# A graph-attention kernel that loads edge features and receivers for two groups of quads at once

## The chip, the cores and the metric

The kernel runs on one core of a Trainium2 chip. The core has a matrix engine (TensorE, called PE in the profile), a vector engine (VectorE, DVE), an activation engine (ScalarE, ACT), a general engine (GpSimd, POOL) and SyncE (SP), which here only issues transfers. Each engine works through its own instructions in order. Transfers run on sixteen DMA engines that all queues share. The metric is the time of one execution on the device, in microseconds (us), lower is better.

## The reference

`x` holds 6250 nodes with 128 features in 8 heads of 16. There are 206250 edges; `src` names the sender and `dst` the receiver, and the edges come sorted by `dst`. The reference is one message-passing layer with a residual and a layer norm:

```
w   = silu(edge_attr_32    @ rad_W1 + rad_b1) @ rad_W2 + rad_b2      # per edge, 128 wide
    + silu(edge_attr_32_n2 @ sph_W1 + sph_b1) @ sph_W2 + sph_b2
q   = (x @ Wq)[dst]         k = (x @ Wk)[src]         v = (x @ Wv)[src]
alpha = sum over a head of (q * w * k) / sqrt(16) * edge_weight      # one per edge and head
out = segment_sum(alpha * v, dst) / 16
result = layernorm(x + out)
```

## The kernel before, in words

**Tiles.** 128 edges are a tile, four tiles a quad (512 edges), four quads a group (2048 edges). There are 101 groups (`NG`) and 403 quads. Because the edges are sorted by receiver, the receivers of one quad lie in a window of 32 nodes, and those of a group in a window of 128. A receiver is kept as its place in the quad's window (`rel`).

**Start.** The kernel computes K and V of every node and stores them as one table in HBM, `kv_tab`, with rows of 1 KB. Beside this it turns `rel` around with TensorE (`relT`), so that the edges of a tile lie along a row, and stores it to HBM: first as `rel_lin`, then, read back with every row repeated four times, as `rel_four` (`store_rel`, lines 477 to 486). `store_rel` is called twice: once for the first 128 tiles (8 groups), early, and once for the rest, at the end of the start. The start also issues the loads for the first groups (lines 541 to 545) and the first gathers.

**The loop** (lines 808 to 881) runs over groups and in each over four slots, one quad a slot, in the order 0, 2, 1, 3. At slot i TensorE computes the first layers of quad i+2 (`first_layers`, line 560, which reads `feats`), the queries at the edges of quad i+1 (line 579, a matmul with the one-hot `hotT`, which DVE makes from `relb`, line 292) and the second layers of quad i+1 (line 612). ACT applies silu (line 597). DVE multiplies q, k and w (lines 628 to 641), and weighs v (line 653). TensorE then sums messages by receiver (line 664).

**K and V rows.** They come by sender from `kv_tab`. Four gathers of 128 rows each on POOL (line 141) bring a quad's rows, issued 14 quads ahead. In 60 of the quads ("row quads", about every 6.55 quads: slots `8 + (n + 1) * 393 // 60`) the fourth tile does not come by a gather: its 128 rows are 128 single transfers of 1 KB into the tile `wide`, 60 issued by SP and 68 by ACT (line 214), after the row addresses have been read into registers (line 208). `load_rows` spreads each row quad's transfers over the slots ahead of it; the last ones stand five slots ahead of the quad in program order. DVE waits for all 128 at line 625 before it starts on the quad at line 628.

**SP's program.** Besides the rows, SP issues for each group: the features `feats` (line 252, 512 KB, in slot 3), the receivers `relb` (line 263, 128 KB, in slot 2), the window of nodes `x` (line 315, 64 KB, in slot 0, behind an address load at line 310 every four groups), and the output `y` (line 773, 64 KB). `feats` has three buffers and `relb` four, and both are loaded three groups ahead. A load of `feats` waits for a signal of TensorE from two slots earlier (`mark`), so that its buffer is free. All of SP's instructions run one after another, so each stands in line with the rows.

Of the kernel before, what the change touches and what calls it, by code (L numbers as in the profile page):

```python
# [12 lines left out]
F32 = mybir.dt.float32  # L13
BF16 = mybir.dt.bfloat16
# [11 lines left out]
P = 128  # L26
# [6 lines left out]
GT = 16  # L33
QT = 4
NQ = GT // QT
NG = math.ceil(E / (P * GT))
NT = NG * GT
EG = P * GT
EQ = P * QT
QUADS = math.ceil(E / EQ)  # L40
NB = math.ceil(N / P)
NBC = 7
ROWS = (NB + 1) * P
W = 32
# [28 lines left out]
def gnn_kernel(ctx, tc, x, src, dst, weight, edges, rad_W1, rad_b1, rad_W2, rad_b2,  # L73
# [14 lines left out]
    nc = tc.nc  # L88
    const = ctx.enter_context(tc.tile_pool(name="const", bufs=1))
    dram = ctx.enter_context(tc.tile_pool(name="dram", bufs=1, space=DRAM))  # L90

    kv_tab = dram.tile([NB * P, 2 * D], F32, name="kv_tab")
    rel_lin = dram.tile([NT, P], BF16, name="rel_lin")
    rel_four = dram.tile([NT // QT, NQ, EQ], BF16, name="rel_four")
    acc = dram.tile([ROWS, D], F32, name="acc")
# [31 lines left out]
    gp = ctx.enter_context(tc.tile_pool(name="group", bufs=2))  # L127
# [45 lines left out]
    feats_of, relb_of, act_of, kv_of, hot_of, hotT_of, x_of, q_of, msg_of = ({} for _ in range(9))  # L173
# [75 lines left out]

    def load_feats(g, mark=None):  # L250
        feats_of[g] = gp.tile([P, EG // 2], F32, name="feats", bufs=3)
        o = nc.sync.dma_start(feats_of[g], edges[g])
        if mark is not None:
            tc.add_manual_dep(o.ins, mark.ins.name, WAIT, reason="one signal of TensorE a quad")
# [3 lines left out]

    def load_rel(g, pool, bufs):

        relb_of[g] = pool.tile([P, EQ], BF16, name="relb", bufs=bufs)
        r = rel_four[g * NQ:(g + 1) * NQ].rearrange("j n e -> (j n) e")
        nc.sync.dma_start(relb_of[g], r[:, None, :].to_broadcast([NQ * NQ, W // NQ, EQ]))

# [74 lines left out]
    with tc.tile_pool(name="nodes", bufs=1) as nodes, \  # L339
# [136 lines left out]

        def store_rel(a, b):
            for i, n in ((slice(a, min(b, NT // P)), P), (slice(NT // P, b), NT % P)):
                if i.start < i.stop:
                    t = slice(i.start * P, i.start * P + (i.stop - i.start) * n)  # L480
                    nc.sync.dma_start(rel_lin[t, :].rearrange("(n p) e -> p n e", p=n), relT[:n, i, :])
            a, b = a * P // QT, min(b * P, NT) // QT
            r = rel_lin.rearrange("(q t) e -> q (t e)", t=QT)
            for a, b in ((a, b - b % (P // 8)), (b - b % (P // 8), b)):
                if a < b:
                    nc.sync.dma_start(rel_four[a:b], r[a:b, None, :].to_broadcast([b - a, NQ, EQ]))

# [13 lines left out]
        n = len(chunks)  # L501
# [17 lines left out]
        for i, (k, n) in enumerate(work):  # L519
# [20 lines left out]
            if i == len(chunks) - 1:  # L540
                load_rel(0, gp, 1)
                load_feats(0)
                for g in range(1, XL):
                    load_x(g)
                    load_feats(g)
                nc.sync.dma_start(scale, weight)
        for q in order[XQ:AHEAD]:
            gathers(q)
        nc.vector.tensor_tensor(bsum, b2[:, 0:1], b2[:, 1:2], op=OP.add)
        store_rel(1, math.ceil(NT / P))  # L550
        nc.vector.tensor_scalar(scale, scale, SCALE, None, op0=OP.mult)


    with tc.tile_pool(name="ps", bufs=1, space=PSUM) as pp, tc.tile_pool(name="loop", bufs=1) as lp:
# [242 lines left out]

        written, ready, ready_at = [], [], []
        load_rel(1, lp, 4)
        load_rel(2, lp, 4)  # L800
        silus(order[0], first_layers(order[0]))
# [6 lines left out]
        for g in range(NG - 1):  # L808
            for slot, j in enumerate((0, 2, 1, 3)):
# [34 lines left out]
                if slot == 0:  # L844
                    if g + XL < NG:
                        load_x(g + XL, past)
                if slot == 3 and g + 3 < NG:
                    load_feats(g + 3, past)
                if slot == 2 and g + 3 < NG:
                    load_rel(g + 3, lp, 4)  # L850
                if slot == 0 and 1 <= g:
# [256 lines left out]
```

## Time and profile before

| | us |
|---|---|
| three runs | 2588.82, 2596.52, 2597.5 (median 2596.52) |
| the profiled execution | 2599.59 |
| its span, first to last instruction | 2597.7 |
| PE busy | 2090.8 |
| DVE busy | 1525.9 |
| POOL busy | 1470.8 |
| ACT busy | 645.0 |

The span is the time from the first to the last instruction of the profiled execution. SP has no busy time in this table, because instructions that issue transfers are not counted as busy; what SP does has to be read from the order of its instructions in time and from what waits for it. The clock that TensorE was granted was 0.837 of full speed on average.

### The profile page before, as it was taken

To read this page: it belongs to the slowest core of one execution; us is meant where nothing else is said; L and a number is where in the kernel's file an instruction comes from. 1 tells how busy PE (TensorE), PEld (TensorE's weight loads), DVE (VectorE), ACT (ScalarE), POOL (GpSimd) and SP (SyncE) were. 2 spreads that over 40 slices of the span, in tenths; PEclk is the share of its full clock that TensorE was granted. 3 is DMA by queue.
4 is the path that set the end of the run, shared out by engine and by line. 5 is a ranking of instruction groups with operands and counts; after the bars stand their busy time and mean duration, and the time that the engine had idled before them with its cause. 6 is when DMAs were issued, how large, how long until landed. Compare 5 with 4: busy or idle time off the path is not lost.

```text
span 2597.7 us, 56700 instructions
## 1 busy us (share of the span) xinstructions
PE 2090.8 (80%) x15990; PEld 1744.9 (67%) x15990; DVE 1525.9 (59%) x3427; ACT 645.0 (25%) x1359; POOL 1470.8 (57%) x1564
## 2 busy tenths in 40 slices
PE   5678888888888788878888878888887888888787
PEld 4567677666767666666667667666766767676666
DVE  3456556656656555656656556555656556565567
ACT  1122222222222222222222222222222222222223
POOL 4456565655565565555556555555555555565540
PEclk7788888888888888888888797888788787887888
DMA  5543444434343343434434434444343343443331
GB/s 180 173 118 112 120 124 116 121 112 122 113 123 116 116 124 114 120 112 122 121 111 123 119 114 121 115 120 121 114 120 118 111 122 115 119 124 108 118 103 35
DMA packets 157219, 307.18 MB, mean 118 GB/s; under 512 B 42022, under 2 KB 91360, under 8 KB 156896
## 3 DMA queue, kind: packets, MB, share of 16 engines
q0 software_dynamic: 73984, 201.43, 27.2%
q1 hardware_dynamic: 72976, 97.35, 11.4%
q10 hardware_dynamic: 9936, 4.72, 0.8%
q8 instruction: 127, 2.08, 0.3%
q14 instruction: 196, 1.61, 0.2%
HBM read 289.88 MB, written 15.11 MB: 117 GB/s over the span
## 4 chain that ended last, share of the span: by engine, by line
PE 38%; issue 20%; SPq 13%; DVE 13%; another core or an unknown queue 10%; ACTq 5%; ACT 1%; DMA 0%; DVEq 0%
PE pw L612 17%; SPq L214 10%; PE pq L579 7%; PE ph L560 6%; ACTq L214 4%; PE po L664 3%; DVE kq L628 3%; DVE side L638 2%; DVE kq L636 2%; SPq L208 2%; PE pq L705 1%; ACT act L597 1%; PE pk L381 1%; PE pq L286 1%
## 5 line engine op out<-in xcount | busy, mean ns | idle before, releaser
L141 POOL DMA_INDIRECT kv<-kv_tab,src_i x1520 | 1436.9, 945 | 1042.9 <-remote 447.9
L612 PE MATMUL pw<-w,act 128*128 128x128 f32 x6448 | 1060.4, 324 | 109.1 <-issue 107.6
L612 PEld LDWEIGHTS pw<-w,act 128*128 128x128 f32 x6448 | 951.7, 231 | 187.0 <-issue 149.7
L597 ACT ACTIVATE act<-ph,b 128x512 f32<-128x512 f32 x806 | 554.7, 689 | 1843.5 <-remote 1374.7
L628 DVE TENSOR_TENSOR kq<-pq,kv 128x512 f32<-128x512 f32 (+1 forms) x404 | 270.6, 670 | 931.3 <-remote 680.0
L560 PE MATMUL ph<-feats,w 32*128 32x512 f32 x1612 | 665.7, 740 | 138.5 <-issue 128.8
L579 PE MATMUL pq<-q,hotT 32*128 32x128 f32 x3224 | 557.5, 321 | 20.9 <-issue 17.8
L579 PEld LDWEIGHTS pq<-q,hotT 32*128 32x128 f32 x3224 | 470.7, 220 | 33.0 <-issue 32.7
L560 PEld LDWEIGHTS ph<-feats,w 32*128 32x128 f32 x1612 | 190.7, 207 | 303.6 <-issue 272.0
L638 DVE TENSOR_REDUCE side<-kq 128x32 f32<-128x512 f32 x404 | 280.2, 694 | 14.0
L653 DVE TENSOR_TENSOR msg<-kv,side 128x512 f32<-128x512 f32 (+1 forms) x404 | 268.7, 665 | 13.9
L636 DVE TENSOR_TENSOR kq<-pw,kq 128x512 f32<-128x512 f32 x404 | 274.1, 679 | 0.0
L664 PE MATMUL po<-msg,hot 128*32 128x128 f32 x3200 | 183.2, 309 | 34.2 <-issue 34.1
L567 PE MATMUL pw<-brow,onesb 3*128 3x512 bf16 x403 | 176.5, 438 | 0.0
L664 PEld LDWEIGHTS po<-msg,hot 128*32 128x32 f32 x3200 | 84.5, 118 | 91.2 <-issue 63.6
L705 PE MATMUL pq<-part,to 128*128 128x128 f32 x196 | 56.6, 380 | 107.6 <-issue 54.4
L705 PEld LDWEIGHTS pq<-part,to 128*128 128x128 f32 x196 | 38.6, 245 | 122.2 <-issue 83.7
L641 DVE TENSOR_TENSOR side<-side,scale 128x32 f32<-128x32 f32 x400 | 79.7, 199 | 13.7
L381 PE MATMUL pk<-wkv,xT 128*128 128x256 f32 x162 | 45.6, 424 | 38.0 <-DVE kv L382 23.9
L292 DVE TENSOR_TENSOR hotT<-relb,side 128x512 f32<-128x512 bf16 x101 | 68.6, 679 | 0.0
L286 PE MATMUL pq<-wq,xT 128*128 128x128 f32 x200 | 49.6, 336 | 23.5 <-issue 15.9
L382 DVE COPY kv<-pk 128x512 f32<-128x512 f32 (+1 forms) x41 | 27.4, 682 | 68.9 <-remote 48.5
(126 smaller groups left out, 892.9 us busy)
## 6 DMA issues: line engine op xcount, KB each, us to landing
wide<-kv_tab ACTq DMA_DIRECT2D x4080, 1.0 KB
wide<-kv_tab SPq DMA_DIRECT2D x3600, 1.0 KB
feats<-in_edges SPq DMA_DIRECT2D x101, 512.0 KB
kv<-kv_tab,src_i POOLq DMA_INDIRECT x1520, 2.9
relb<-rel_four SPq DMA_DIRECT2D x101, 128.0 KB
x<-in_x SPq DMA_DIRECT2D x101, 64.0 KB
out<-y SPq DMA_DIRECT2D x101, 64.0 KB
kv_tab<-kv SPq DMA_DIRECT2D x12, 512.0 KB
```

The costliest lines, as they stand in the source:

```text
L141: return nc.gpsimd.indirect_dma_start(out=o, out_offset=None, in_=table, in_offset=bass.IndirectOffsetOnAxis(ap=index, axis=0))
L214: signalled(engine.dma_start(row_of[q][p:p + 1, 0, :].bitcast(U8), table[:, ds(regs.pop(p), ROW_BYTES)]))
L560: return nc.tensor.matmul(act_of[q, i], w1[r0:r0 + R, :], feats_of[g][r0:r0 + R, c0:c0 + EQ], start=True, stop=True)
L567: nc.tensor.matmul(pw, onesb[f:f + 3, :], brow[f:f + 3].rearrange("p t d -> p (t d)"), start=True, stop=False)
L579: o = nc.tensor.matmul(pq_of[q][:, t, :], hotT_of[g][b, t * P:(t + 1) * P], q_of[g][b, :], start=True, stop=True)
L597: o = nc.scalar.activation(act, act_of[q, i], AF.Silu, bias=b1[:, i:i + 1])
L612: o = nc.tensor.matmul(pw[:, t, :], act_of[q, i][:, t * P:(t + 1) * P], w2[:, i, :], start=False, stop=(t == QT - 1 and i == 1))
L628: o = nc.vector.tensor_tensor(kq_of[q][:, u, :], pq_of[q][:, u, :], kv[:, :, :D], op=OP.mult)
L636: nc.vector.tensor_tensor(m, pw_of[q][:, t, :], m, op=OP.mult)
L638: nc.vector.tensor_reduce(alpha, m.rearrange("p t (h e) -> p t h e", e=HD), AX.X, OP.add)
L653: nc.vector.tensor_tensor(msg_of[q][:, u, :].rearrange("p t (h e) -> p t h e", e=HD), kv[:, :, D:].rearrange("p t (h e) -> p t h e", e=HD) ...
L664: o = nc.tensor.matmul(po_of[g][j * W:(j + 1) * W, :], hot_of[g][:, j * QT + t, :], msg_of[g * NQ + j][:, t, :], start=(t == 0), stop=(t = ...
```

## The change

`feats` and `relb` are loaded for two groups (a pair) with one transfer each. A feature tile is now 128 x 2 x 1024 numbers (1 MB) with two buffers, a receiver tile 128 x 1024 numbers (256 KB) with two buffers in the loop; in the loop both are issued only in odd groups, in the slots where they stood. To make a pair's receivers one stretch for each row, `rel_lin` and `rel_four` are laid out by pairs: `rel_lin` holds even and odd groups apart, and `rel_pair` replaces `rel_four`. `store_rel` now counts in pairs; its first call covers one pair, its second the other 50.

```diff
-    rel_lin = dram.tile([NT, P], BF16, name="rel_lin")
-    rel_four = dram.tile([NT // QT, NQ, EQ], BF16, name="rel_four")
+    rel_lin = dram.tile([2, PAIRS, GT, P], BF16, name="rel_lin")
+    rel_pair = dram.tile([PAIRS, NQ, NQ, 2, EQ], BF16, name="rel_pair")
...
-    def load_feats(g, mark=None):
-        feats_of[g] = gp.tile([P, EG // 2], F32, name="feats", bufs=3)
-        o = nc.sync.dma_start(feats_of[g], edges[g])
+    def pair_of(u):
+        return range(2 * u, min(2 * u + 2, NG))
+
+    def load_feats(u, mark=None):
+        pair = pair_of(u)
+        feats = gp.tile([P, 2, EG // 2], F32, name="feats")
+        for g in pair:
+            feats_of[g] = feats[:, g - pair[0], :]
+        o = nc.sync.dma_start(feats[:, :len(pair), :],
+                              edges[pair[0]:pair[-1] + 1].rearrange("g p e -> p g e"))
...
-    def load_rel(g, pool, bufs):
-
-        relb_of[g] = pool.tile([P, EQ], BF16, name="relb", bufs=bufs)
-        r = rel_four[g * NQ:(g + 1) * NQ].rearrange("j n e -> (j n) e")
-        nc.sync.dma_start(relb_of[g], r[:, None, :].to_broadcast([NQ * NQ, W // NQ, EQ]))
+    def load_rel(u, pool, bufs):
+
+        pair = pair_of(u)
+        n = len(pair) * EQ
+        relb = pool.tile([P, 2 * EQ], BF16, name="relb", bufs=bufs)
+        for g in pair:
+            relb_of[g] = relb[:, (g - pair[0]) * EQ:(g - pair[0] + 1) * EQ]
+        r = rel_pair[u].rearrange("j n h e -> (j n) (h e)")[:, :n]
+        nc.sync.dma_start(relb[:, :n], r[:, None, :].to_broadcast([NQ * NQ, W // NQ, n]))
...
-        def store_rel(a, b):
-            for i, n in ((slice(a, min(b, NT // P)), P), (slice(NT // P, b), NT % P)):
-                if i.start < i.stop:
-                    t = slice(i.start * P, i.start * P + (i.stop - i.start) * n)
-                    nc.sync.dma_start(rel_lin[t, :].rearrange("(n p) e -> p n e", p=n), relT[:n, i, :])
-            a, b = a * P // QT, min(b * P, NT) // QT
-            r = rel_lin.rearrange("(q t) e -> q (t e)", t=QT)
-            for a, b in ((a, b - b % (P // 8)), (b - b % (P // 8), b)):
-                if a < b:
-                    nc.sync.dma_start(rel_four[a:b], r[a:b, None, :].to_broadcast([b - a, NQ, EQ]))
+        def store_rel(c, d):
+
+            ends_at = [min(d, (NG + 1 - h) // 2) for h in range(2)]
+            for u in range(c, min(c + NQ, d)):
+                for h, e in enumerate(ends_at):
+                    p, n = u % NQ * 2 * GT + h * GT, len(range(u, e, NQ))
+                    nc.sync.dma_start(
+                        rel_lin[h, u:e:NQ].rearrange("n m e -> m n e"),
+                        relT[p:p + GT, u // NQ:u // NQ + n, :])
+            for h, e in enumerate(ends_at):
+                r = rel_lin[h].rearrange("u (j t) e -> (u j) (t e)", t=QT)
+                m = e - (e - c) % NQ
+                for x, y in ((c, m), (m, e)):
+                    if x < y:
+                        nc.sync.dma_start(
+                            rel_pair[x:y, :, :, h, :].rearrange("u j n e -> (u j) n e"),
+                            r[x * NQ:y * NQ, None, :].to_broadcast([(y - x) * NQ, NQ, EQ]))
...
                 for g in range(1, XL):
                     load_x(g)
-                    load_feats(g)
+                load_feats(1)
...
-        store_rel(1, math.ceil(NT / P))
+        store_rel(1, PAIRS)
...
-        load_rel(1, lp, 4)
-        load_rel(2, lp, 4)
+        load_rel(1, lp, 2)
...
-                if slot == 3 and g + 3 < NG:
-                    load_feats(g + 3, past)
-                if slot == 2 and g + 3 < NG:
-                    load_rel(g + 3, lp, 4)
+                if slot == 3 and g % 2 == 1 and g + 3 < NG:
+                    load_feats((g + 3) // 2, past)
+                if slot == 2 and g % 2 == 1 and g + 3 < NG:
+                    load_rel((g + 3) // 2, lp, 2)
```

The instructions of PE, DVE, ACT and POOL stand in the same order in both programs; only SP's program differs, at the start and in the loop.

In the loop, SP's rows over about two groups stand so before (`wide` is the tile that the single rows go to, `at_i` the table of their addresses, `gb_i` that of the windows of `x`):

```order
L315 DMA x<-in_x 128x512
L214 DMA wide<-kv_tab 1x1024 x2
L208 TENSOR_LOAD at_i
L214 DMA wide<-kv_tab 1x1024 x17
L263 DMA relb<-rel_four 128x1x512
L214 DMA wide<-kv_tab 1x1024 x11
L252 DMA feats<-in_edges 128x1024
L208 TENSOR_LOAD at_i
L214 DMA wide<-kv_tab 1x1024 x5
L315 DMA x<-in_x 128x512
L214 DMA wide<-kv_tab 1x1024 x20
L263 DMA relb<-rel_four 128x1x512
```

The same place on SP in the changed program:

```order
L327 DMA x<-in_x 128x512
L215 DMA wide<-kv_tab 1x1024 x2
L209 TENSOR_LOAD at_i
L215 DMA wide<-kv_tab 1x1024 x17
L275 DMA relb<-rel_pair 128x1x1024
L215 DMA wide<-kv_tab 1x1024 x11
L259 DMA feats<-in_edges 128x2x1024
L209 TENSOR_LOAD at_i
L215 DMA wide<-kv_tab 1x1024 x5
L327 DMA x<-in_x 128x512
L215 DMA wide<-kv_tab 1x1024 x27
L209 TENSOR_LOAD at_i
```

The first `relb` and `feats` stand where they stood, for two groups now; those of the next group are gone, and the rows there follow one another without them.

At the end of the start, SP's second store of the receivers and what follows it, before, with the semaphores that each waits for (`DMAHW` are eight completion counters of transfers used in turn; `Activation` and `PE` are signals of those engines):

```order
L481 DMA rel_lin<-relT 128x11x128 [waits DMAHW6_49,Activation_49]
L481 DMA rel_lin<-relT 80x128 [waits DMAHW7_49,Activation_49]
L486 DMA rel_four<-rel_lin 1472x1x512 [waits DMAHW7_49,DMAHW6_49,DMAHW0_49]
L486 DMA rel_four<-rel_lin 16x1x512 [waits DMAHW1_49]
L263 DMA relb<-rel_four 128x1x512 [waits DMAHW2_49,PE_49]
L263 DMA relb<-rel_four 128x1x512 [waits DMAHW3_49]
L315 DMA x<-in_x 128x512 [waits DMAHW4_49,PE_49]
```

The same place on SP in the changed program, from the fifth of the eight stores of `rel_lin` on:

```order
L495 DMA rel_lin<-relT 16x12x128 [waits DMAHW3_49]
L495 DMA rel_lin<-relT 16x12x128 [waits DMAHW4_49]
L495 DMA rel_lin<-relT 16x12x128 [waits DMAHW5_49]
L495 DMA rel_lin<-relT 16x12x128 [waits DMAHW6_49]
L503 DMA rel_pair<-rel_lin 768x1x512 [waits DMAHW5_49,DMAHW7_49,DMAHW3_49,DMAHW1_49]
L503 DMA rel_pair<-rel_lin 32x1x512 [waits DMAHW0_49]
L503 DMA rel_pair<-rel_lin 768x1x512 [waits DMAHW6_49,DMAHW4_49,DMAHW2_49]
L503 DMA rel_pair<-rel_lin 16x1x512
L275 DMA relb<-rel_pair 128x1x1024 [waits DMAHW7_49,DMAHW1_49,PE_49]
L327 DMA x<-in_x 128x512 [waits PE_49]
```

Two stores of `rel_lin` became eight and two of `rel_four` became four; two loads of `relb` became one, and that one now waits (counters 7 and 1) until both long stores of `rel_pair` have landed, since the first call of `store_rel` no longer covers its groups.

More of the change, by code (lines that the diff above doesn't have):

```diff
@@ L40 @@
 QUADS = math.ceil(E / EQ)
+PAIRS = math.ceil(NG / 2)
 NB = math.ceil(N / P)
```

## The prediction

> **What bounds the kernel now.** I read the page's chain first, then the chain of single stretches, the waits of SP's own queue, the instructions on the tile `wide`, and last SP in order of time. The chain names PE most, but also SP's queue, though SP computes nothing:
>
> ```profile
> PE 38%; issue 20%; SPq 13%; DVE 13%; another core or an unknown queue 10%; ACTq 5%; ACT 1%; DMA 0%; DVEq 0%
> ```
>
> These are averages. The chain of 1080 to 1160 us and that of 2410 to 2505 us:
>
> ```profile
> by line: SPq L214 47.3%; issue 35.8%; SPq L208 10.7%; SPq L773 2.6%; SPq L315 1.4%; SPq L252 1.4%; SPq L263 0.8%; another core or an unknown queue 0.0%; SPq L310 0.0%
> ```
>
> ```profile
> by line: SPq L214 44.0%; issue 40.5%; SPq L208 9.6%; SPq L773 1.6%; SPq L315 1.4%; SPq L252 1.4%; SPq L263 1.3%; SPq L310 0.1%
> ```
>
> There the chain is SP alone: it issues the single rows (L214), and L252 and L263, which the change halves, stand in the same line. Does SP ever wait? The waits of SP's queue between 300 and 2580 us, longest first:
>
> ```profile
> SPq L773 <- DMA out<-y: 6.5, 5, 1.6
> SPq L773 <- ACT act L597: 1.7, 4, 0.5
> SPq L315 <- remote: 0.9, 5, 0.2
> ...
> ```
>
> With the smaller ones that is under 13 us of 2280: SP has work all the time. Whether it is also late shows on the row quads. The instructions on `wide` (DVE, first and last start of a stretch), for 200 to 523, 320 to 490 and 520 to 2548 us:
>
> ```profile
> L628 DVE TENSOR_TENSOR kq<-pq,wide x9: 279/280/281, 206.5 to 522.2; 128x128 f32<-128x128 f32 x9
> ```
>
> ```profile
> L628 DVE TENSOR_TENSOR kq<-pq,wide x5: 280/280/281, 328.4 to 484.8; 128x128 f32<-128x128 f32 x5
> ```
>
> ```profile
> L628 DVE TENSOR_TENSOR kq<-pq,wide x51: 278/280/281, 522.2 to 2546.9; 128x128 f32<-128x128 f32 x51
> ```
>
> By line 148 the fourth and the eighth row quad stand at slots 34 and 60, the first, ninth and 59th at 14, 66 and 394. So early a quad takes (484.8 - 328.4) / 26 = 6.015 us, or (522.2 - 206.5) / 52 = 6.07 with the uneven first ones; later (2546.9 - 522.2) / 328 = 6.173. Where the later time goes is seen in DVE in order of time, an early row quad and a late one with the quad behind it:
>
> ```profile
> 405.93 0.56 DVE L628 TENSOR_TENSOR kq<-pq,kv 128x384 f32<-128x384 f32 x1 [0.98 <-PE pq L579]
> ```
>
> ```profile
> 2349.36 0.56 DVE L628 TENSOR_TENSOR kq<-pq,kv 128x384 f32<-128x384 f32 x1 [6.97 <-issue]
> ...
> 2354.59 0.69 DVE L628 TENSOR_TENSOR kq<-pq,kv 128x512 f32<-128x512 f32 x1 [1.60 <-PE pq L579]
> ```
>
> The late row quad stood 7 us, the early one 1 us. So SP starts with a lead, loses it, and in the late stretch a row quad can stand for SP's last rows. The most that relief of SP can bring is the difference of pace over those 328 quads: 328 x (6.173 - 6.015) = 52 us. That is the **cap**.
>
> **The change, part by part.** *Half of the loads go.* 101 loads of `feats` become 51, 101 of `relb` 51: 50 each leave SP. Their price in a quick stretch of SP (start, length, line, count):
>
> ```profile
> 1090.00 1.56 SPq L214 DMA_DIRECT2D wide<-kv_tab  x5
> 1091.66 0.36 SPq L252 DMA_DIRECT2D feats<-in_edges  x1
> 1092.12 3.62 SPq L214 DMA_DIRECT2D wide<-kv_tab  x10
> ```
>
> ```profile
> 1160.01 3.49 SPq L214 DMA_DIRECT2D wide<-kv_tab  x11
> 1163.55 0.56 SPq L263 DMA_DIRECT2D relb<-rel_four  x1
> 1164.20 1.42 SPq L214 DMA_DIRECT2D wide<-kv_tab  x4
> ```
>
> A row takes 0.33 us (3.49 for ten steps and one length of about 0.23), 0.10 of it the gap ahead. From the end of the rows before to the start of the row behind, `feats` takes 1092.12 - 1091.56 = 0.56, less that gap 0.46 us; `relb` 1164.20 - 1163.50 = 0.70, less the gap 0.60. Together 1.06 us, times 50: 53 us. In a slow stretch it is more:
>
> ```profile
> 1133.13 6.46 SPq L214 DMA_DIRECT2D wide<-kv_tab  x12
> 1140.31 0.70 SPq L252 DMA_DIRECT2D feats<-in_edges  x1
> 1141.72 6.25 SPq L214 DMA_DIRECT2D wide<-kv_tab  x11
> ```
>
> Here `feats` takes 1141.72 - 1139.59 = 2.1 us. Were all as dear, 50 pairs of loads would be over 100 us, far beyond the cap. I take the quick price: SP is quick while the loop stands at a row quad, and it is that standing that gets shorter.
>
> *What remains gets longer.* A pair load moves twice the bytes, for `feats` in two pieces a partition. Does a longer load cost more to issue? `feats` (512 KB) and `x` (64 KB), shortest, middle and longest in ns:
>
> ```profile
> L252 SPq DMA_DIRECT2D feats<-in_edges x101: 3/359/757, 71.4 to 2549.4; - x101
> ```
>
> ```profile
> L315 SPq DMA_DIRECT2D x<-in_x x101: 3/356/793, 57.9 to 2536.8; - x101
> ```
>
> Eight times the bytes, the same 0.36 us. The shape can matter: `relb`, with one more dimension, took 0.56. The pair of `relb` keeps its shape: 0. The pair of `feats` gets a dimension: between 0 and 0.46 (nothing saved); I take 0.2, the step from 0.36 to 0.56, times 50: 10 us. SP's relief is 53 - 10 = 43 us, under the cap. The Trainium skill, page "DMA: Bandwidth & Descriptors", section "Issuing engines are not separate DMA queues", speaks against any such gain: what spreading issues over engines saves is only the sequencer's time to initiate a transfer, which it calls "usually small relative to the DMA itself". By that rule the sum would be 0 in place of 43. The trace differs at this kernel: 0.33 us a row, without a wait, is what the chain consists of.
>
> *The rows behind a load.* A pair load brings 1 MB into the queue in which the rows stand. SP behind a `feats`, and behind an `x` right after:
>
> ```profile
> 183.67 0.19 SPq L252 DMA_DIRECT2D feats<-in_edges  x1
> 184.40 5.48 SPq L214 DMA_DIRECT2D wide<-kv_tab  x10
> 189.93 0.68 SPq L315 DMA_DIRECT2D x<-in_x  x1
> 190.64 9.13 SPq L214 DMA_DIRECT2D wide<-kv_tab  x17
> ```
>
> 0.55 us a row behind 512 KB, 0.54 behind 64 KB: size does not slow SP. I take 0; the other end is a rival below. The total of bytes is unchanged.
>
> *Buffers and signals.* Loads of odd groups stay where they were with the same signal of TensorE; those of the next group come four slots earlier with them. Nothing new is awaited in the loop: 0. DVE and PE wait for 50 landings fewer each; neither stood at them: 0.
>
> *The start.* SP and POOL:
>
> ```profile
> 64.45 0.66 SPq L486 DMA_DIRECT2D rel_four<-rel_lin  x1
> ...
> 109.51 1.09 SPq L481 DMA_DIRECT2D rel_lin<-relT  x2
> 112.42 1.47 SPq L486 DMA_DIRECT2D rel_four<-rel_lin  x2
> 114.01 1.22 SPq L263 DMA_DIRECT2D relb<-rel_four  x2
> 123.62 0.38 SPq L315 DMA_DIRECT2D x<-in_x  x1
> ```
>
> ```profile
> 75.24 0.94 POOL L141 DMA_INDIRECT kv<-kv_tab,src_i  x1 [31.73 <-DMA feats<-in_edges]
> ```
>
> ```profile
> 120.00:125.00 5.00, 5.00 (x29) 4.78 (x30) 0.00 (x0) 1.18 (x2) 0.94 (x1) 0.53 0.04 12
> ```
>
> The first store gets two transfers more (0.66 and about 0.4), ahead of five stores of `kv_tab` that the first gather at 75.24 waits for: 0 to 1 us, I take 1. The second gets eight for two (8 x 0.55 = 4.4 us for 1.1) and four for two (2.9 for 1.5), 4.7 us in all, and the next `relb` now waits for the stores to land. They had landed by 120 (the row above: DMA share 0.04 from 120 to 125); 4 to 5 us later is 125, where SP would else have stood until 123.62 for a signal. So `x` of group 3 comes 1 to 2 us later, its use a group later: 0 to 1, I take 0.5. The first pair has to land for these, in order:
>
> ```profile
> L292 DVE TENSOR_TENSOR hotT<-relb,side x101: 676/678/681, 76.7 to 2568.5; 128x512 f32<-128x512 bf16 x101
> ```
>
> ```profile
> L560 PE MATMUL ph<-feats,w x1612: 584/692/1218, 114.3 to 2575.0; 32*128 32x512 f32 x180
> ```
>
> The first `relb` is issued at 70.5 and used at 76.7, and DVE's time there lies under the gathers; `feats`, issued at 71.4, is first used at 114.3. Hidden.
>
> **Sum.** 2599.6 - 53 + 10 + 1.5 = 2558. The profiled execution lies 3.1 above the median of the runs, 2596.5; so the median should become 2555.
>
> **Rivals.**
> *B, another pace takes over.* If the pace without SP is 6.07 and not 6.015, the cap is 328 x (6.173 - 6.07) = 34 us, and some row quads still wait for ACT's rows (5% of the chain) or for a lump of SP's: 8 to 25 us are left, about 2580. For it: the uneven first quads are quads too. Against: they have the start to recover from.
> *C, no change.* SP's shares of the chain are made of waits that PE's own pace would fill. Then 2596.5 + 1.5 = 2598. For it: PE is busy 80%. Against: 6.015 against 6.173 with the same PE work. The Trainium skill's rule above leads here too.
> *D, slower: a pair load holds SP.* What moves when 512 KB of `feats` land (us, then PE, PEld, DVE, ACT, POOL, clock, DMA share, GB/s):
>
> ```profile
> 1092.70:1093.70 1.00, 1.00 (x8) 0.78 (x5) 0.76 (x3) 0.24 (x1) 0.00 (x1) 0.50 0.93 324
> 1093.70:1094.70 1.00, 1.00 (x6) 1.00 (x6) 1.00 (x2) 1.00 (x3) 0.94 (x1) 0.50 0.45 174
> ```
>
> The DMA engines are nearly full for one to two us. With 1 MB it would be two us more, and if the queue takes no more rows while these move, each pair load costs 2.0 us where two loads cost nothing beyond their issue: 50 x 2.0 - 53 = 47 us slower, some 2645. It decides at 53 / 50 = 1.06 us a pair load. Against: the rows went in at 0.36 us each during just that transfer (3.62 for ten). The Trainium skill, same page, section "Queues, rings and completion order", states that each DMA engine takes its descriptors in ring order, so a row behind a pair load would land later, without saying that SP is held; no row here times a single landing.
>
> **Chances.** The sum's case 0.52 (2537 to 2572: from the cap with some slow-stretch prices to a dear `feats`), B 0.20 (2572 to 2589), C 0.11, D 0.17. The range, 2535 to 2602, holds the first three. Below 0.3% (8 us) this kernel's runs, which lie 9 us apart, can't tell a change. Faster by more: 0.52 + 0.20 = 0.72; within: 0.11; slower: 0.17.
>
> **What would show it.** L259 and L275 stand 51 times each. Right: row quads at 39.4 to 39.7 us in the late stretch (40.5 before), SP's queue under 7% of the chain, DVE's standing at row quads down to 1 to 3 us. The issue of the pair of `feats` at 0.4 to 0.6 us. The first gather no later than 76.5. Wrong: row quads unchanged with SP's rows further apart behind L259 (D), or SP waiting while the pace stays (C).

## The result and the profile after

The changed kernel takes 2566.26 us (median of five runs, 2561.54 to 2572.61) against 2596.71 (five runs, 2588.82 to 2599.69): a ratio of 0.9886, 95% interval 0.9862 to 0.9909, or 30 us faster: 1.1%, small, but clear of the scatter. The profiled execution of the changed kernel took 2561.54 us, 4.7 below the median; the one of before lay 3.1 above the median it is compared with in the prediction. So the two profiles lie 38 us apart where the medians lie 30 apart.

The head of the page of the changed kernel:

```profile
span 2559.8 us, 56497 instructions
...
PE 2074.7 (81%) x15990; PEld 1730.3 (68%) x15990; DVE 1526.5 (60%) x3427; ACT 644.7 (25%) x1359; POOL 1474.4 (58%) x1564
```

PE, DVE, ACT and POOL execute as many instructions as before, and all of them are busy for nearly the same time. The chain of waits of this execution breaks off at its last instruction, so SP's share of it can't be compared; the rest is read from other views.

**Where the 38 us lie.** DVE's instructions on the tile `wide` (first and last start), of the changed kernel for 198 to 520, 320 to 482, 516 to 1515 and 1510 to 2510 us:

```profile
L647 DVE TENSOR_TENSOR kq<-pq,wide x9: 278/280/280, 202.6 to 518.2; 128x128 f32<-128x128 f32 x9
...
L647 DVE TENSOR_TENSOR kq<-pq,wide x5: 278/280/280, 323.9 to 480.8; 128x128 f32<-128x128 f32 x5
...
L647 DVE TENSOR_TENSOR kq<-pq,wide x26: 278/280/281, 518.2 to 1512.6; 128x128 f32<-128x128 f32 x26
...
L647 DVE TENSOR_TENSOR kq<-pq,wide x26: 278/280/281, 1512.6 to 2507.5; 128x128 f32<-128x128 f32 x26
```

The same tile in the kernel before, the late stretch in its two halves:

```profile
L628 DVE TENSOR_TENSOR kq<-pq,wide x26: 278/280/281, 522.2 to 1536.5; 128x128 f32<-128x128 f32 x26
...
L628 DVE TENSOR_TENSOR kq<-pq,wide x26: 278/280/281, 1536.5 to 2546.9; 128x128 f32<-128x128 f32 x26
```

The span splits at the first, the ninth and the 59th row quad:

| part | before, us | after, us | difference |
|---|---|---|---|
| start, to the first row quad shown | 206.5 | 202.6 | -3.9 |
| first to ninth row quad (52 quads) | 315.7 | 315.6 | -0.1 |
| ninth to 59th row quad (328 quads) | 2024.7 | 1989.3 | -35.4 |
| rest of the span | 50.8 | 52.3 | +1.5 |

Nearly all of the gain is in the late stretch: (2507.5 - 518.2) / 328 = 6.065 us a quad in place of 6.173, so that a row quad comes every 39.8 us. The early quads take what they took, 6.07.

**DVE's standing at row quads.** Idle time of DVE ahead of its first multiplication, by what ended it (sum, times, longest). The kernel before, 520 to 1512 and 1537 to 2548 us:

```profile
DVE kq L628 <- DMA wide<-kv_tab: 25.0, 5, 6.5
DVE kq L628 <- issue: 14.1, 3, 6.4
DVE kq L628 <- DVEq L625: 8.4, 2, 4.3
...
DVE kq L628 <- DVEq L625: 35.7, 9, 6.4
...
DVE kq L628 <- DMA wide<-kv_tab: 18.8, 3, 7.1
DVE kq L628 <- issue: 18.4, 3, 7.0
```

The changed kernel, all rows of 516 to 1512 us, and the rows of 1512 to 2508 us that tell of rows (L644 is the wait for the 128 rows):

```profile
DVE kq L647 <- remote: 327.0, 135, 2.9
DVE kq L647 <- PE pq L598: 36.2, 18, 6.1
...
DVE kq L647 <- DVEq L644: 22.5, 7, 6.3
DVE kq L647 <- issue: 17.5, 3, 7.3
DVE kq L647 <- DMA wide<-kv_tab: 17.1, 4, 6.7
```

Before, 47.5 us were stood in the first half and 72.9 in the second. After, nothing is stood in the first half and 57.1 in the second. SP's lead, worked out from the trace as the time between the issue of its last row of a row quad and DVE's start on that quad, tells why: before it was 28 us at first and under 5 us from the 14th row quad (about 720 us) on; after, it is about 20 us still at 1000 us, and falls to 5 us only at the 32nd row quad (about 1430 us); from there on it is 1 to 6 us (7.6 at the very last). SP still loses its lead, but takes twice as long to.

**What the standing costs.** The second half stands 57 us more than the first, and takes the same time, 994.9 us against 994.4. So is standing free? To see it, I split each half by quads: from DVE's start on the quad ahead of a row quad to its start on the quad behind the row quad (two quads, 25 times a half), and all other quads (114 a half, from start to start; worked out from the traces, one execution of each kernel).

| us | before, 1st half | after, 1st half | before, 2nd half | after, 2nd half |
|---|---|---|---|---|
| the two quads at a row quad | 11.98 | 11.20 | 12.37 | 11.72 |
| each other quad | 6.27 | 6.27 | 6.15 | 6.16 |

The other quads take the same in both kernels; in the second half they are quicker in both, because it ends with four quads after the last gather (gathers run 14 quads ahead), and these take 4.0 us on average. All of the gain stands in the first row: 25 x (11.98 - 11.20) = 19.5 us and 25 x (12.37 - 11.72) = 16 us. Where no row quad stands it is 11.20, so the 57 us that the changed kernel still stands in its second half cost it 25 x (11.72 - 11.20) = 13 us. A row quad that stood is followed by a quicker quad (into the row quad 6.6 us and the next one 5.1, in place of 5.1 and 6.1), so most of the standing is made up, but not all. Without any standing for rows, the 328 quads would by this take 1989 - 13 = 1976 us, or 6.02 us a quad.

**SP.** The pair loads (shortest, middle, longest in ns), and SP's longest waits from 300 to 2580 us:

```profile
L259 SPq DMA_DIRECT2D feats<-in_edges x51: 3/401/1511, 69.1 to 2510.5; - x51
```

```profile
L275 SPq DMA_DIRECT2D relb<-rel_pair x51: 3/561/1199, 67.9 to 2505.7; - x51
```

```profile
SPq L792 <- DMA out<-y: 6.9, 5, 2.1
SPq L925 <- POOL y L920: 3.9, 2, 3.0
SPq L1123 <- PEq L1123: 3.1, 2, 2.4
```

Twice the bytes cost 0.04 us more to issue (`feats`, 0.401 against 0.359) and 0.02 (`relb`, 0.561 against 0.539). SP still has work nearly all the time. What it spends that time on, from its last row of the first row quad to its last row of the 60th (each instruction counts until the next one starts, the semaphore waits of the loads with them; worked out from the traces):

| SP, us | loads of `feats` and `relb` | 3540 rows | the rest | sum |
|---|---|---|---|---|
| before | 101.3 (96 of each) | 1901.3 | 390.5 | 2393.1 |
| after | 52.9 (48 of each) | 1922.1 | 383.4 | 2358.4 |

The loads give back 48.4 us, and 20.8 of that goes into the rows, which are as many as before but take a little longer each. A cause can be seen in the same traces: from one row to the next SP takes 0.66 to 0.67 us while POOL's gathers run and 0.33 while POOL pauses, in both kernels. When DVE stands less for rows, POOL pauses less: its pauses of more than 2.5 us sum to 120 us before and 62 after. That fits the dearer rows; no run isolates it, and the rows of the executions of the third round below differ by up to 10 us among themselves.

**The start.** SP in order of time, and the first gather on POOL:

```profile
62.08 1.48 SPq L503 DMA_DIRECT2D rel_pair<-rel_lin  x2
63.65 4.12 SPq L399 DMA_DIRECT2D kv_tab<-kv  x5
67.88 1.20 SPq L275 DMA_DIRECT2D relb<-rel_pair  x1
69.13 0.73 SPq L259 DMA_DIRECT2D feats<-in_edges  x1
...
106.86 3.79 SPq L495 DMA_DIRECT2D rel_lin<-relT  x8
111.75 2.66 SPq L503 DMA_DIRECT2D rel_pair<-rel_lin  x4
120.03 0.54 SPq L275 DMA_DIRECT2D relb<-rel_pair  x1
120.68 1.42 SPq L327 DMA_DIRECT2D x<-in_x  x1
```

```profile
72.50 0.95 POOL L142 DMA_INDIRECT kv<-kv_tab,src_i  x1 [29.55 <-DMA relb<-rel_pair]
```

The first gather starts 2.7 us earlier than before, in spite of the added stores, and DVE starts on the first quad at 113.7 us in place of 118.2. In the four runs of the third round below it was 117 to 119 us, with the start of either kernel, so this is scatter of the start and not the change. The stores of the second call go out in 7.6 us, and the `relb` behind them waits from 114.4 to 120.03; nobody waits for it.

### The profile page after: what moved, and what is told of

It reads as the page before. It is cut to its first block, busy times and chain, and to the rows that moved or that the text cites. A ratio compares the mean times of both kernels' runs of the same rounds, so it can differ in the third digit from the quotient of the medians.

```text
span 2559.8 us, 56497 instructions
## 1 busy us (share of the span) xinstructions
PE 2074.7 (81%) x15990; PEld 1730.3 (68%) x15990; DVE 1526.5 (60%) x3427; ACT 644.7 (25%) x1359; POOL 1474.4 (58%) x1564
## 5 line engine op out<-in xcount | busy, mean ns | idle before, releaser
L598 PE MATMUL pq<-q,hotT 32*128 32x128 f32 x3224 | 550.6, 318 | 11.4 <-DVE kq L647 8.4
L598 PEld LDWEIGHTS pq<-q,hotT 32*128 32x128 f32 x3224 | 464.2, 217 | 17.6 <-issue 17.2
L309 DVE TENSOR_TENSOR hot<-rel,side 128x512 f32<-128x512 f32 x100 | 67.9, 679 | 0.0
```

The lines of the kernel that those rows point to most:

```text
L598: o = nc.tensor.matmul(pq_of[q][:, t, :], hotT_of[g][b, t * P:(t + 1) * P], q_of[g][b, :], start=True, stop=True)
```

## The experiments

The theory: SP is late in the late stretch, and each instruction it doesn't issue brings the rows forward by its issue time, until the loop's own pace takes over. Rivals: it is the landing of the transfers, their number of bytes or their bunching, that matters, and not the issue; or a pair load itself holds SP and gives part of the gain back; or only one of the two pairs matters.

### First round: each part alone, on another chip

Four kernels. *Only `feats` by pairs* (the rest as before):

```diff
+    def load_feats(u, mark=None):
+        pair = pair_of(u)
+        feats = gp.tile([P, 2, EG // 2], F32, name="feats")
...
-                if slot == 3 and g + 3 < NG:
-                    load_feats(g + 3, past)
+                if slot == 3 and g % 2 == 1 and g + 3 < NG:
+                    load_feats((g + 3) // 2, past)
```

> Only the features are loaded by pairs; receivers and their tables stay as before. Theory (SP's time to issue is what the change saves): 50 loads of feats at 0.46 us less about 0.05 us for the longer ones leave SP, some 20 us of SP's time, so 2576 to 2586 against 2597. Rival (longer transfers use the DMA engines better): relb, whose rows grow from 1 KB to 2 KB, would carry the gain, and feats, whose pieces stay 4 KB, would give nothing: 2593 to 2600.

*Only `relb` by pairs* (the changed kernel with `feats` one group at a time):

```diff
-                if slot == 3 and g % 2 == 1 and g + 3 < NG:
-                    load_feats((g + 3) // 2, past)
+                if slot == 3 and g + 3 < NG:
+                    load_feats(g + 3, past)
```

> Only the receivers are loaded by pairs, from the table ordered by pairs; features stay single. Theory (SP's time to issue): 50 loads at 0.60 us, 30 us of SP's time, most of it gained until the loop's own pace holds: 2569 to 2580. Rival (better use of the DMA engines by 2 KB rows): all of the gain, 2562 to 2570.

*Two small loads in the place of the two removed ones* (the changed kernel; 16 KB each, into a tile that nothing reads):

```diff
+                if slot in (2, 3) and g % 2 == 0 and g + 3 < NG:
+                    nc.sync.dma_start(pad[:, slot - 2, :], x[:P, :32])
```

> The changed kernel, with two small transfers (16 KB each, into a tile that nobody reads) on SP in each even group, in the two slots from which a load was taken. Theory (number of instructions on SP): the gain goes, 2588 to 2600. Rival (size and number of the large transfers): nothing changes, 2562 to 2572, since the loads themselves stay paired.

*The changed kernel's tiles, table and places, but each pair by two transfers back to back:*

```diff
-        o = nc.sync.dma_start(feats[:, :len(pair), :],
-                              edges[pair[0]:pair[-1] + 1].rearrange("g p e -> p g e"))
+        for g in pair:
+            o = nc.sync.dma_start(feats_of[g], edges[g])
...
-        nc.sync.dma_start(relb[:, :n], r[:, None, :].to_broadcast([NQ * NQ, W // NQ, n]))
+        for g in pair:
+            h = slice((g - pair[0]) * EQ, (g - pair[0] + 1) * EQ)
+            nc.sync.dma_start(relb[:, h], r[:, None, h].to_broadcast([NQ * NQ, W // NQ, EQ]))
```

> Tiles, tables and places as in the changed kernel, but each pair is loaded by two transfers, one right behind the other, as many on SP as before. Theory (number of instructions on SP): as before, 2590 to 2602. Rival (loads are rarer and further ahead, half of the slots are free of them): most of the gain stays, 2564 to 2580. If bunching 1 MB holds the rows, slower than before, over 2605.

All four expectations count from 2597 us. On the chip that these ran on, the kernel before takes 1972.49 us (16 runs, 1970.76 to 1976.45), 24% less for the same program.

| kernel | us | ratio to before | 95% interval |
|---|---|---|---|
| only `feats` by pairs | 1984.96 | 1.0061 | 1.0042 to 1.0079 |
| only `relb` by pairs | 1971.69 | 1.0001 | 0.9992 to 1.0011 |
| small loads for the removed | 1999.14 | 1.0131 | 1.0114 to 1.0148 |
| two by two | 1980.31 | 1.0034 | 1.0021 to 1.0048 |

Nothing gains here, and the kernels with a pair of `feats` in one tile are 0.3% to 1.3% slower. This round doesn't test the theory for the chip of the prediction; it says that the gain hangs on what bounds the loop, and that on this chip it is something else.

### Second round: what bounds the loop on such a chip

The next runs fell on a third chip, of the same kind (before: 1974.31 us, 7 runs). The changed kernel again, as it is:

> The changed kernel itself, beside the one before on the chip of this job. On the chip of the first comparison (before: about 2597 us) SP's issuing was late and the change gained 1.1%. Where the kernel before takes about 1972 us, SP's last rows are issued 13 to 20 us ahead of their use and wait about 8 us in their queue. Theory (SP's time to issue): there, less time to issue gains nothing, ratio 0.997 to 1.006, the more since feats by pairs alone gave 1.006; on a chip like the first one, 0.985 to 0.992. Rival (a pair load is the better transfer anywhere): about 0.99 on either.

It took 1978.06 us, ratio 1.0016 (1.0002 to 1.0030), in the range expected for such a chip. The kernel before, for its trace:

> The kernel before itself, for its trace on the chip of this job. If the chip is one where it takes about 2597 us, row quads come every 40.5 us from the ninth on and SP's last row of a tile is issued 1.5 to 5 us ahead of its use; if one of about 1972 us, every 31 us, 13 to 20 us ahead. The rival (SP is late everywhere) has less than 5 us on both.

It took 1973.35 us. Row quads come every 31.0 us from the ninth on, as expected, and SP's last row is issued 15 to 33 us ahead, somewhat more than expected. Its gathers on POOL (busy, mean ns, idle time ahead and what ended it), against the same row of the kernel before on the chip of the prediction:

```profile
L141 POOL DMA_INDIRECT kv<-kv_tab,src_i x1520 | 1440.0, 947 | 464.1 <-issue 394.8 <-DVE kq L628 11.6 <-DVE msg L653 10.4
```

```profile
L141 POOL DMA_INDIRECT kv<-kv_tab,src_i x1520 | 1436.9, 945 | 1042.9 <-remote 447.9 <-issue 352.0 <-PE pq L579 170.8
```

On the third chip POOL issues the 1520 gathers without a break, one every 1.25 us (0.947 and a gap of 464.1 / 1520 = 0.305): 1904 of a span of 1971.6 us. On the chip of the prediction it has 579 us more of idle time between them. The rows of the gathers on the faster chips, first and last start, of the kernel before, of the changed one and of that with small loads:

```profile
L141 POOL DMA_INDIRECT kv<-kv_tab,src_i x1520: 942/947/1712, 44.1 to 1946.9; - x190
```

```profile
L142 POOL DMA_INDIRECT kv<-kv_tab,src_i x1520: 942/946/1401, 45.0 to 1945.8; - x190
```

```profile
L143 POOL DMA_INDIRECT kv<-kv_tab,src_i x1520: 942/946/1720, 44.1 to 1944.8; - x190
```

The gathers end at 1945.6 to 1947.9 us in every kernel of these two rounds; what differs is how far the loop trails behind them. From the end of the last gather to the end of the span it is 23.7 us in the kernel before, 24.3 with only `relb` by pairs, 30.6 in the changed kernel, 34.1 two by two, 35.1 with only `feats` by pairs, 51.8 with the small loads. So on these chips the stream of gathers is the floor, which the kernel before reaches, and relief of SP has nothing to bring. Two more runs test that by taking SP's lateness away altogether: four rows a row quad go from SP to ACT, in the kernel before and in the changed one.

```diff
-ROW_ACT = 68
+ROW_ACT = 72
...
-    at_i = const.tile([ROW_TILES, P + 4], I32, name="at_i")
+    at_i = const.tile([ROW_TILES, P + 8], I32, name="at_i")
```

> The kernel before with four rows of each row quad moved from SP to ACT (56 on SP, 72 on ACT): 240 rows leave SP, at 0.33 us each 79 us of its time, and ACT, which issues its last rows 17 us ahead, takes them. Theory (SP late): on a chip of about 2597 us a gain up to the loop's own pace, that is like the changed kernel or a little more: ratio 0.983 to 0.990. On one of about 1972 us 0.995 to 1.005. Rival (the paired transfers, not SP's time, made the gain): 0.997 to 1.003 on both.

> The changed kernel with the same four rows moved to ACT. Theory with a cap: on a chip of about 2597 us the loop already runs near its own pace, 6.06 us a quad, so only 0 to 6 us more than the changed kernel, ratio 0.984 to 0.989. Rival (no cap, every microsecond that leaves SP is gained): 79 us more, ratio about 0.96.

The kernel before with this edit took 1973.02 us, ratio 0.9992 (0.9978 to 1.0006); the changed one 1989.17, ratio 1.0083 (1.0067 to 1.0098). DVE's waits from 300 to 1900 us, of the kernel before without the edit and with it:

```profile
DVE kq L628 <- DVEq L625: 174.4, 71, 7.2
DVE kq L628 <- PE pq L579: 135.4, 131, 2.8
```

```profile
DVE kq L628 <- PE pq L579: 285.8, 244, 3.1
...
DVE kq L628 <- DVEq L625: 0.8, 1, 0.8
```

SP's longest waits in the kernel with the edit, 300 to 1900 us:

```profile
SPq L252 <- PE pq L579: 166.1, 77, 5.0
SPq L315 <- PE pq L579: 32.5, 44, 2.1
```

174 us of standing at the wait for rows go away, SP's waits of these two kinds grow from 25 us to 199, and the time stays where it was. What follows: standing at row quads is no price where another stream sets the end, here the gathers. What remains open is why the loop trails further with the pair of `feats`. In the changed kernel the row quads take 6.41 us where they took 6.02, and quads away from rows the same (4.34 and 4.35; averages worked out from the traces for quads 20 to 267); with 72 rows on ACT, where no quad stands for rows, the changed kernel still trails 38.5 us against 22.7, spread over all quads. One candidate shows in the traces: on the third chip the row that SP issues right behind a pair of `feats` begins to move 16.9 us after its issue (middle of 48), where a row behind a single `feats` (second chip, only `relb` by pairs) does so after 14.4 (middle of 95); SP's last rows are issued 13 to 23 us ahead of their use, so that can make a row quad stand. It doesn't explain the 38.5 us, where none stands. So the cause stays open.

These two kernels were meant for a chip like the first as well (0.983 to 0.990 and 0.984 to 0.989 were expected there) and ran on no such chip.

### Third round: SP made late on purpose, on a chip like the first

These ran on a chip where the kernel before takes 2596.87 us (7 runs, 2593.6 to 2603.52). SP gets 72 of the 128 rows in place of 60, so that it is late by far in each kernel (its last row of a row quad is issued 1.6 to 1.7 us ahead of DVE's start, in the middle, as before and changed) and no other pace can cap what its relief brings:

```diff
-ROW_ACT = 68
-ROW_AT = {SP: 0, ACT: 64}
+ROW_ACT = 56
+ROW_AT = {SP: 0, ACT: 72}
```

The kernel before with this edit:

> SP is made late on purpose: the kernel before with 72 rows of each row quad on SP and 56 on ACT (60 and 68 before), and so a third address load for each. 720 rows and 60 address loads more on SP, about 300 to 400 us of its time. On chips of about 1973 us, where SP has little to spare, 2150 to 2400; this is the base for the three beside it.

The changed kernel with it:

> The changed kernel with the same 72 and 56. Theory (each load that leaves SP gives back its time to issue while SP is late): 50 pairs of loads at 1.06 us, less up to 10 us for the longer ones, and no cap here: 40 to 55 us under the base. Rival (SP is held by bytes and pieces in its queue, not by the number of instructions): within 10 us of the base, since bytes and pieces are as many.

Two by two with it:

> Pair tiles, the table by pairs and the places of the changed kernel, but two transfers for each pair, one right behind the other, with the same 72 and 56. Theory: as many instructions on SP as in the base, so within 8 us of it. Rival (the gain is from loads that are rarer and further ahead, or from the table): like the changed kernel, 40 us or more under the base. If 1 MB at once holds the rows: over the base.

Only `relb` by pairs with it:

> Only the receivers by pairs, features single, with the same 72 and 56. Theory: 50 loads of relb at 0.60 us, 25 to 32 us under the base, which leaves 13 to 23 for the features. Rival (2 KB rows in place of 1 KB): all of the changed kernel's gain.

| kernel, 72 rows on SP | us | range of 4 runs | against the first |
|---|---|---|---|
| as before | 2869.0 | 2861.48 to 2878.98 | |
| changed (both by pairs) | 2810.3 | 2804.15 to 2814.92 | -58.7 |
| two by two | 2878.85 | 2878.22 to 2879.23 | +9.9 |
| only `relb` by pairs | 2837.95 | 2830.81 to 2845.44 | -31.0 |

Against the kernel before as it is, the ratios are 1.1063 (1.1032 to 1.1094), 1.0816 (1.0792 to 1.0840), 1.1087 (1.1069 to 1.1106) and 1.0928 (1.0899 to 1.0958); the intervals of two of them leave about 10 us on a difference. SP waits for less than 14 us in each of the four. DVE's group in part 5 of the page, as before and changed (busy, mean ns, idle ahead and what ended most of it):

```profile
L628 DVE TENSOR_TENSOR kq<-pq,kv 128x512 f32<-128x512 f32 (+1 forms) x404 | 270.3, 669 | 1196.7 <-remote 550.9
```

```profile
L647 DVE TENSOR_TENSOR kq<-pq,kv 128x512 f32<-128x512 f32 (+1 forms) x404 | 270.3, 669 | 1149.2 <-remote 538.4
```

The row quads over the whole program, as before, changed, two by two, and only `relb` by pairs:

```profile
L628 DVE TENSOR_TENSOR kq<-pq,wide x60: 278/280/281, 205.2 to 2841.5; 128x128 f32<-128x128 f32 x60
```

```profile
L647 DVE TENSOR_TENSOR kq<-pq,wide x60: 278/280/282, 206.1 to 2794.8; 128x128 f32<-128x128 f32 x60
```

```profile
L649 DVE TENSOR_TENSOR kq<-pq,wide x60: 278/280/282, 205.4 to 2858.5; 128x128 f32<-128x128 f32 x60
```

```profile
L643 DVE TENSOR_TENSOR kq<-pq,wide x60: 278/280/282, 204.9 to 2819.8; 128x128 f32<-128x128 f32 x60
```

The first row quad stands at 205 to 206 us in all four, so what differs lies in the loop. The same bytes in the same tiles at the same places by two transfers (third) give nothing, by one each (second) they give 58.7 us. Bytes, tiles and places are thus out. One rival is left: a pair of `relb` also moves its bytes in half as many pieces of 2 KB, and two by two undoes that together with the number of instructions. SP's own time decides it, counted as in the table of SP above (here 4248 rows):

| SP, us | loads of `feats` and `relb` | rows | sum |
|---|---|---|---|
| as before | 103.2 | 2120.8 | 2652.1 |
| changed | 59.8 | 2119.7 | 2604.5 |
| two by two | 109.5 | 2121.2 | 2672.3 |
| only `relb` by pairs | 70.9 | 2129.4 | 2631.5 |

The loads give back 43.4 us, the rows take the same to 1.1 us, and the profiled executions of the two kernels lie 46.6 us apart (2859.7 and 2813.1 us of span). So it is SP's time for the instructions themselves, and not bytes, pieces or bunching. Per pair of loads removed the gain of the medians is 58.7 / 50 = 1.17 us, of which `relb` has 31.0 / 50 = 0.62 and `feats` the remaining 27.7 / 50 = 0.55, each uncertain by about 0.2; by SP's own time it is 43.4 / 48 = 0.90.

Against what was expected: the base costs 272 us more than the kernel before, under the 300 to 400; the changed kernel's 58.7 lies just above 40 to 55; two by two is 9.9 over the base where within 8 was expected, which the scatter covers; `relb` alone, 31.0, lies in 25 to 32, and what it leaves for `feats`, 27.7, above 13 to 23.

## Why the prediction was right, and what it mis-sized

The forecast was 2555 us, 2535 to 2602, with faster at 0.72; the median is 2566, 11 above the forecast, and faster. By its steps:

- **What bounds.** Right: SP had no time to spare and its rows ended the wait of row quads. The third round shows it as a cause and not as a share of a chain: the same loads issued two by two give the gain back (2878.85 against 2810.3).
- **Price of the removed loads** (53 us at the quick price). Right: SP's own time for the two loads fell by 48.4 us in the profiled pair, for 48 of the 50 pairs and with the longer loads in it. The slow-stretch price of over 2 us a pair of loads was not paid.
- **The dearer pair of `feats`** (10 us taken). Mis-sized: its issue takes 0.401 us against 0.359, 0.04 x 50 = 2 us. So the relief was about 48 us and not 43.
- **The cap** (52 us). Near, though from a narrow base: four early row quads gave 6.015 us a quad, the same place gives (480.8 - 323.9) / 26 = 6.035 in the changed kernel, where DVE stands for no rows in either. By the split above, a late stretch without standing takes 1976 us, which is a cap of 2024.7 - 1976 = 49.
- **From relief to gain.** This is the step that failed. The prediction booked SP's relief whole as gain because it was under the cap. Of 48 us of relief 35 were gained in the loop. In the first half the changed kernel stands for no rows at all; there relief beyond the 19.5 us could bring nothing. In the second half SP has lost its lead again, and row quads still cost 13 us by their standing. And SP's rows took 20.8 us more: the prediction noted that SP is quick while the loop stands, but set at nothing that less standing makes its rows dearer.
- **Errors that met.** The sum asked for -53 + 10 + 1.5 = -41.5 us, the profiled executions lie -38 apart: -35.4 in the late stretch, -3.9 in the start, where +1.5 was expected and the scatter is 5, and +1.4 in the remainder. The profiled execution, at 2561.5, so came out 3.5 above the sum's 2558. The rest of the 11 us is that this execution is the quickest of its five, 4.7 below their median, while 3.1 had been allowed for on the other side. A relief taken too small and a gain taken as whole offset each other, and the start added 4 us by chance: the closeness is partly luck. The range held the time with room.
- **Rival B** (another pace takes over, 6.07, a cap of 34 us, of which 8 to 25 are left). The late stretch's 6.065 looks like B's pace and its gain, 35.4, like B's cap, but 13 us lost at row quads are still in it, so that is no pace of the loop alone. What B said of row quads that still wait for SP came true.
- **Rows behind a load, and rival D** (a pair load holds SP). Taken as 0, and right for SP: in the changed kernel of the third round it issues the four rows behind a pair of `feats` at 0.51 us each, where any four rows take 0.62 each, and a pair load in place of two gained 0.90 to 1.17 us, so nothing of D's 2.0 us shows. The Trainium skill, page "DMA: Bandwidth & Descriptors", section "Queues, rings and completion order", says that each DMA engine takes its descriptors in ring order; by that rule the rows behind a pair load land later. The trace agrees: the packet of the row right behind a pair of `feats` starts 3.5 us after its issue (middle of 48), behind a single `feats` 2.1 (`relb` by pairs alone), of any row 0.6. What that cost DVE isn't separated here; on balance the pair loads gained.
- **Rival C and the rule behind it** (no change). Falls on the chips with 2597 us. The Trainium skill, same page, section "Issuing engines are not separate DMA queues", calls the sequencer's time to initiate a transfer "usually small relative to the DMA itself"; by that rule the 100 loads less would have brought nothing. The trace disagrees: 100 issues were worth 58.7 us where SP was late. On the two chips with 1973 us, C is what happened (1.0016 for the changed kernel), though by another mechanism than C's: there POOL's gathers set the end.
- **The start** (+1.5 us). Measured -3.9, with a scatter of 5 us between executions, so neither shown nor refuted. The first gather came at 72.5, before the 76.5 allowed.
- **Signs announced.** L259 and L275 stand 51 times: right. Row quads at 39.4 to 39.7 us: 39.8, just outside. DVE standing 1 to 3 us at row quads: right in the first half only; in the second single row quads still stand up to 7.3 us. Issue of the pair of `feats` at 0.4 to 0.6: 0.401. SP's share of the chain can't be read.

## What to carry to other kernels

A relief of the engine that is late is worth its issue time times its count where the engine is late all the way: with 72 rows on SP, 43 us less of loads on SP went with 47 us less of span. Where it is late in one stretch and ahead in another, ask for each stretch how much standing there is to remove and whether the relief suffices: here 48 us of relief brought 35, since one half had no more standing to give and the other still had some. Ask too whether the engine's other work gets dearer when the loop stands less. To learn what such a change is worth apart from all this, make the engine later on purpose in both kernels and compare them. And idle time at one place isn't yet a price: compare the quads around it with quads that didn't stand. Here 57 us of standing in one half cost about 13, and 174 us on another chip nothing, because the work behind made it up or another stream set the end.

## What the runs showed of the hardware

**One program, two times.** The kernel before takes 2597 us in the first comparison and in the third round, and 1972 to 1974 on the two chips of the rounds between. The gathers in order of time on POOL, from 700 us, on the chip of the prediction:

```profile
699.74 0.94 POOL L141 DMA_INDIRECT kv<-kv_tab,src_i  x1 [1.67 <-remote]
700.99 0.94 POOL L141 DMA_INDIRECT kv<-kv_tab,src_i  x1 [0.30 <-issue]
702.24 0.94 POOL L141 DMA_INDIRECT kv<-kv_tab,src_i  x1 [0.30 <-issue]
703.48 0.95 POOL L141 DMA_INDIRECT kv<-kv_tab,src_i  x1 [0.31 <-issue]
705.90 0.94 POOL L141 DMA_INDIRECT kv<-kv_tab,src_i  x1 [1.47 <-remote]
```

Here POOL, ACT and DVE start again together about 1.2 to 1.5 us after the fourth gather of a quad has ended (704.43 to 705.90 for POOL; ACT at 705.66 after 4.35 us of idle time), though by the trace the last matmul ahead of the pause had ended at 704.36 and those that ACT and DVE follow by 702.2. A quad during which four gathers are issued takes 6.2 us, and one with three, the quad ahead of an early row quad, 4.75. On the faster chips the gathers run through at 1.25 us and the other engines don't start in step with them; quads away from rows (no row quad, nor one of the two behind it) take 4.35 us on average. In the first fortieth of the span the DMA engines move 180 GB/s on the one and 333 on the other. What sets the two chips apart isn't known from these runs; nothing in the programs differs.

**Landing of single rows.** A transfer of one row of 1 KB on ACT's queue landed about 0.95 us after its issue on the chip of the prediction and about 8 us after it on the faster chips, while the middle packet took 0.046 us on both (worked out from the traces). The quicker chip is the one with the later landing.

**Issue beside gathers.** On the chip of the prediction SP goes from one row to the next in 0.66 us on average while POOL's gathers run and in 0.33 while POOL pauses; on the faster chips, where the gathers never pause, it takes 0.37 to 0.40. What stretches SP's steps on the one chip and not on the others isn't known from these runs.

**Issue hardly depends on size.** SP takes 0.36 us to issue 64 KB or 512 KB and 0.40 us for 1 MB in two pieces a partition.
